# First layer of a two-layer selective scan: states in pairs, softplus passes ahead of the pairs, old y added at the copy

## The chip, the cores and the metric

One core of one Trainium2 chip runs the whole program. The metric is the device time of one execution in microseconds (us). A program on one core is compared by the medians of several executions; the profile is of one further execution of the same kernel.

## The reference, cut to what matters

The input is x, four images of 64 x 64 positions with 192 channels. Two layers follow each other; the change is in the first. It normalizes x, projects it to u (384 channels) and a gate z, and runs a selective scan over the 4096 positions in four directions (by rows, by columns, and both backwards). In each direction there are 384 channels with 16 states each:

```python
def step(h, inp):
    dt, ut, bt, ct = inp
    dA = jnp.exp(dt[..., None] * A_k[None])
    dBu = dt[..., None] * bt[:, :, None, :] * ut[..., None]
    h = dA * h + dBu
    y = jnp.einsum('bkdn,bkn->bkd', h, ct)
    return (h, y)
```

Here dt is the softplus of a small projection, and bt and ct (16 numbers each for every position) are projections too. The four directions' y are summed at their positions, u times D is added, and the sum is normalized, gated with silu(z), projected back to 192 channels and added to x.

## The kernel before, in words

The first layer works image by image ("batch" b = 0 to 3). `between` finishes the image before and projects the next; `scans` (from line 572) does the four directions of one image. The change lies wholly in `scans`.

**Tiling.** An item is one direction k (0 and 2 by rows, forward and backward; 1 and 3 by columns) and one chunk of 512 of the 4096 positions. There are 32 items in an image: first 16 with k = 0 and 2, then 16 with k = 1 and 3. Directions 0 and 2 alternate, and so do 1 and 3. Each item has 16 steps, n = 0 to 15, one for each state; a step works on all 384 channels, as three blocks d of 128 channels on the partitions. All steps of an image make one list `flat`, and g counts through it (512 steps, 2048 in the program).

**What one step does.** For state n of an item:

- ACT makes xT = dt * u * b_n with positions on the partitions (`b_product`, line 716, four ACTIVATE) and the decay a = exp(A dt) (`decay`, line 728, three ACTIVATE).
- PE turns xT, block by block, so that channels lie on the partitions (`turn_x`, line 733; four transposes of 128 x 128 for each d, into one of three PSUM buffers x).
- DVE runs h = a h + x along the 512 positions (`scan`, line 741; three scans of 128 x 512), each starting from the last column of the item before in that direction. After the third, a `tensor_reduce` (line 751) copies the three last columns into the tile carry.
- POOL multiplies h by the row c_n, spread over the partitions by DMA as bct (`c_product`, line 755; 128 x 1536, in place).
- PE turns the product back and adds it in PSUM to the three banks yp (`add_y`, line 768; twelve transposes with accumulation).

**Order.** Each engine's program is written out by hand: the loop over g issues, for every step, first ACT's work for later steps (`b_product(g + 2)`, `decay(g + 1)`), then for d = 0, 1, 2 the scan, the transposes of x for step g + 1 and the adds into y of a state three steps back (LAG = 3), and then the product by c. So on PE an add of state g - 3 stands between the transposes of x for step g + 1. After an item begins, the adds of its first states wait until n = 4, and two states are then added in one step.

**Preparing later items.** Item.steps (line 685) spreads the making of dt and of dt * u for the next two items over the 16 steps: line (ahead, n, engine, function). PE computes dt's projection twice (`dt_rows`, 13 rows into 512 columns; for the item two ahead in steps 7 to 9, for the next item in steps 5 to 7), ACT takes the absolute value and the exponential (steps 10 to 13), POOL has four passes of 128 x 1536: `plus` after the product of step 14 and `minus` after that of step 15 (for the item two ahead), `rest` after the product of step 1 and `total` after that of step 4 (for the next item). ACT takes the logarithm at step 2. DVE forms dt from a PSUM result and these (`delta`, line 661, steps 7 to 9) and dt * u (`times_u`, line 681, steps 11 to 13). In the first eight items of an image the gate's projection is fitted in too (PE and ACT, steps 13 to 15 and following).

**Old y.** The directions are summed in DRAM. Before an item's first add, PE seeds the three banks yp with the old y by a matmul with the identity (`start_y`, line 762: at n = 3 for two banks, n = 4 for the third). The old y of the next item is loaded (tile yold, one buffer) at step 5; only where the next item goes from rows to columns (17th item) is it loaded after the last store of the item before. When an item is done, DVE copies the three banks to the tile yt (`end_y`, line 781) in steps 2 and 3 of the next item, and SP stores yt.

**Buffers.** h has seven tiles of 128 x 1536 (pool b7), a, xT and bct three each, yold, yt, e, wl one each, carry two for each state and direction pair. SP issues all these DMAs in one queue.

Of the kernel before, what the change touches and what calls it, by code (L numbers as in the profile page):

```python
# [12 lines left out]
ALU = mybir.AluOpType  # L13
# [389 lines left out]
class FirstLayer:  # L403
# [168 lines left out]
    def scans(self):  # L572
        nc, tc = self.tc.nc, self.tc
        with ExitStack() as ctx:
            pool = lambda name, bufs, **k: ctx.enter_context(tc.tile_pool(name=name, bufs=bufs, **k))
            p1, p2, p3, p7 = pool("b1", 1), pool("b2", 2), pool("b3", 3), pool("b7", 7)
            pk = pool("ca", 2)
            ps_y = pool("psy", 1, space=bass.MemoryType.PSUM)
            ps_x = pool("psx", 3, space=bass.MemoryType.PSUM)
# [7 lines left out]
            def last(ap, k):  # L587
                return ap[..., LC - 1 : LC] if k < 2 else ap[..., 0:1]
# [15 lines left out]
            class Item:  # L604
# [80 lines left out]
                def steps(self):  # L685

                    s = lambda f, *a: (lambda: f(*a))
                    r = [(3, 12, "pool", self.load_rows), (2, 0, "pe", self.turn_b), (2, 1, "dve", self.keep_b)]
                    for d in range(ND):
                        r += [(2, 7 + d, "pe", s(self.dt_rows, d)), (2, 10 + d, "act", s(self.absolute, d))]  # L690
                    r += [(2, 13, "act", self.exp), (2, 14, "pool", self.plus), (2, 14, "pool", self.load_u)]
                    r += [(2, 15, "pool", self.minus), (1, 2, "act", self.log)]
                    r += [(1, 1, "pool", self.rest), (1, 4, "pool", self.total)]
                    for d in range(ND):
                        r += [(1, 5 + d, "pe", s(self.dt_rows, d)), (1, 7 + d, "dve", s(self.delta, d))]
                    for b in range(ND):
                        r += [(1, 10 + b, "pe", s(self.turn, b)), (1, 11 + b, "dve", s(self.times_u, b))]
                    return r
# [8 lines left out]
                    items += pair if i < NCH // 2 else pair[::-1]  # L707
            flat = [(it, n) for it in items for n in range(NS)]
            N = len(flat)
            carry, xTs, xs, as_, hs, cs = {}, {}, {}, {}, {}, {}  # L710

            def b_product(g):
                it, n = flat[g]
# [22 lines left out]

            def scan(g, d):
                it, n = flat[g]
                if d == 0:
                    hs[g] = p7.tile([128, ND, LC], F32, name="h")  # L740
                nc.vector.tensor_tensor_scan(  # L741
                    along(hs[g][:, d, :], it.k),
                    along(as_[g][:, d, :], it.k),
                    along(xs.pop((g, d)), it.k),
                    0.0 if it.first else carry[it.k, n][:, d : d + 1],
                    ALU.mult,
                    ALU.add,
                )
                if d == ND - 1:
                    kept = carry[it.k, n] = pk.tile([128, ND], F32, name=f"carry{it.k // 2}_{n}")  # L750
                    nc.vector.tensor_reduce(kept, last(hs[g], it.k), mybir.AxisListType.X, ALU.max)  # L751

            def c_product(g):
                it, n = flat[g]
                nc.gpsimd.tensor_tensor(hs[g], hs[g], bc(cs[g - n % 2][:, n % 2, :], 1, ND), ALU.mult)  # L755

            def start_y(it, b):

                if b == 0:
                    it.yp = [ps_y.tile([128, LC], F32, name=f"yp{i}") for i in range(ND)]  # L760
                yo = it.yold.rearrange("p j e -> p (j e)")[:, b * LC : (b + 1) * LC]
                nc.tensor.matmul(it.yp[b], ident, yo, start=True, stop=False, skip_group_check=True)  # L762

            def add_y(g, b):
                it, n = flat[g]
                for i in range(NJ):
                    j, d = divmod(b * NJ + i, ND)
                    nc.tensor.matmul(  # L768
                        it.yp[b][:, i * 128 : (i + 1) * 128],
                        hs[g][:, d, j * 128 : (j + 1) * 128],  # L770
                        ident,
                        start=False,
                        stop=n == NS - 1,
                        is_transpose=True,
                        skip_group_check=True,
                    )

            def end_y(it, b):
                if b == 0:
                    it.yt = p1.tile([128, NJ, DI], F32, name="yt")  # L780
                nc.vector.tensor_copy(it.yt.rearrange("p j e -> p (j e)")[:, b * LC : (b + 1) * LC], it.yp[b])
                if b == ND - 1:
                    for of, to in rows(it.yt, self.y_dram, it.k, it.c):
                        nc.sync.dma_start(to, of)
# [13 lines left out]
            with tc.manual_schedule(engines={nc.tensor.engine, nc.scalar.engine, nc.vector.engine, nc.gpsimd.engine}):  # L798
                tc.keep_in_program_order(nc.scalar.preload_act_table_set("natural_log_exp_and_others"))
                plan = {}  # L800
                for i, it in enumerate(items):
                    for ahead, n, engine, f in it.steps():
                        if i < ahead:
                            f()
                        else:
                            plan.setdefault((i - ahead) * NS + n, []).append((engine, f))
                for t in range(NCH):
                    for e in range(ND):
                        plan.setdefault(t * NS + 13 + e, []).append(("pe", lambda t=t, e=e: gate_in(t, e)))
                        plan.setdefault(t * NS + 15 + e, []).append(("act", lambda t=t, e=e: gate_out(t, e)))  # L810

                def prepare(g, engine):
                    for e, f in plan.get(g, []):
                        if e == engine:
                            f()

                items[0].yold = load("yold", self.y_dram, items[0].k, items[0].c)
                c_rows(0)
                b_product(0)
                b_product(1)  # L820
                decay(0)
                for d in range(ND):
                    turn_x(0, d)
                LAG = 3
                late = []
                for g in range(N + LAG + 1):
                    i, n = divmod(g, NS)
                    it = items[i] if g < N else None
                    before = items[i - 1] if i > 0 else None
                    prepare(g, "act")  # L830
                    if g + 2 < N:
                        if g % 2 == 0:
                            c_rows(g + 2)
                        b_product(g + 2)
                    if g + 1 < N:
                        decay(g + 1)
                    adds = [[] for _ in range(ND)]
                    if it is not None:
                        for at, b in (((LAG, 1), 0), ((LAG, 2), 1), ((LAG + 1, 0), 2)):
                            if at[0] == n:  # L840
                                adds[at[1]].append((start_y, it, b))

                    ready = [x for x in late if x <= g - LAG and (n > LAG or x // NS < i)][:2]
                    for j, (x, b) in enumerate((x, b) for x in ready for b in range(ND)):
                        adds[j // len(ready)].append((add_y, x, b))
                    late = [x for x in late if x not in ready]
                    for d in range(ND):
                        if g < N:
                            scan(g, d)
                        if d == 1:  # L850
                            prepare(g, "dve")
                        if before is not None and (n, d) in ((LAG - 1, 2), (LAG, 0), (LAG, 1)):
                            end_y(before, {2: 0, 0: 1, 1: 2}[d])
                            if (n, d) == (LAG, 1) and it is not None and it.yold is None:
                                it.yold = load("yold", self.y_dram, it.k, it.c)
                        if g + 1 < N:
                            turn_x(g + 1, d)
                        for f, *a in adds[d]:
                            f(*a)
                    if g < N:  # L860
                        prepare(g, "pe")
                        c_product(g)
                        late.append(g)
                        prepare(g, "pool")
                        if n == 5 and i + 1 < len(items) and items[i + 1].k % 2 == it.k % 2:
                            q = items[i + 1]
                            q.yold = load("yold", self.y_dram, q.k, q.c)


    def finish(self, batches):  # L870
# [762 lines left out]
```

## Time and profile before

| | |
|---|---|
| median of 3 executions | 11105.2 us (11085.83 to 11113.26) |
| the profiled execution | 11106.54 us |
| its span, first to last instruction | 11104.6 us |
| granted TensorE clock, mean | 0.939 |
| the four scan stages of the first layer | about 2200 us each, 8793 us together |
| busy over the span | PE 86%, DVE 87%, ACT 88%, POOL 77% |
| scans (L741) | 6144 of 128 x 512, mean 1266 ns (768 without carry: 1207 ns) |
| products by c (L755) | 2048, mean 3470 ns |
| reduces (L751) | 2048, mean 158 ns |
| softplus passes on POOL | 128 each: plus 1478, minus 1482, rest 3460, total 3477 ns |
| seeding of y (L762) | 768 matmul records, 445.1 us busy |
| copies of y (L781) | 384, mean 674 ns |

The page gives for each group of instructions the line, the engine, the operation, what is written and read, the count, the busy time, the mean duration and the idle time of the engine just before it with the instruction that ended it. PE computes in fp32, and a matmul of 512 columns leaves two records. Instructions of one engine overlap a little at their ends, so that the distance from start to start is shorter than the mean duration: five products by c in a row take 17.12 us, 3.42 each. The chain of waits at the end of the span lies in the second layer, and tells nothing of the scan stage; there one reads a window of the timeline instead.

### The profile page before, as it was taken

The page shows a single profiled execution, that of the slowest core. Times are in us where ns is not written, and L with a number is a line of the kernel's source. Part 1 is how long each engine was busy: PE and PEld are TensorE (multiplying, and loading weights), DVE is VectorE, ACT ScalarE, POOL GpSimd, SP SyncE. Part 2 cuts the span into 40 slices and gives each one's busy share as a digit, 9 for nine tenths or more (in the row PEclk, how much of TensorE's full clock was granted, in tenths as well). Part 3 has the DMA queues.
Part 4 walks back from the last instruction along what each step waited for, and adds up shares of the span by engine and source line. Part 5 has one row for each costly group of instructions (what it writes and reads, how often), then busy time and mean ns, then how long its engine had stood idle before and what let it go on. Part 6 is the DMA issues. An engine that isn't in the chain of part 4 may idle for free. (4 is left out here: it accounts for less than half of the span.)

```text
span 11104.6 us, 172135 instructions
## 1 busy us (share of the span) xinstructions
PE 9551.9 (86%) x61449; PEld 7273.6 (66%) x61449; DVE 9693.3 (87%) x11515; ACT 9775.8 (88%) x16979; POOL 8587.9 (77%) x2776
## 2 busy tenths in 40 slices
PE   7998888888988888888988888889988888788677
PEld 4776666666776666656776666657766766655366
DVE  4999899976999899968999899949998999878675
ACT  5999999977999999969999999959999999856477
POOL 3999899955999899938999899929998999700370
PEclk8999999998999999998999999989999999989688
DMA  4333344344333344443333433353333434433458
GB/s 125 109 108 101 91 101 101 98 137 127 109 106 101 92 101 99 98 159 112 109 103 96 98 97 99 93 168 109 109 99 95 98 98 98 120 119 123 157 131 272
DMA packets 833671, 1267.54 MB, mean 114 GB/s; under 512 B 102026, under 2 KB 517655, under 8 KB 832292
## 3 DMA queue, kind: packets, MB, share of 16 engines
q1 hardware_dynamic: 827940, 1250.15, 40.5%
q0 software_dynamic: 4864, 6.29, 0.4%
q8 instruction: 488, 8.00, 0.3%
q14 instruction: 379, 3.10, 0.1%
HBM read 955.83 MB, written 300.42 MB: 113 GB/s over the span
## 5 line engine op out<-in xcount | busy, mean ns | idle before, releaser
L755 POOL TENSOR_TENSOR h<-h,bct 128x1536 f32<-128x1536 f32 x2048 | 7062.9, 3470 | 579.9 <-DVE carry L751 477.5
L741 DVE TENSOR_TENSOR_SCAN h<-a,carry,x 128x512 f32<-128x512 f32 x5376 | 6604.9, 1266 | 231.0 <-PE x L733 194.9
L733 PE MATMUL x<-ident,xT 128*128 128x128 f32 x24576 | 4000.8, 287 | 811.8 <-DVE h L741 710.1
L716 ACT ACTIVATE xT<-dtuT,bT 128x384 f32<-128x384 f32 x8192 | 4358.8, 609 | 93.0 <-PE x L733 87.3
L733 PEld LDWEIGHTS x<-ident,xT 128*128 128x128 f32 x24576 | 2804.0, 145 | 2136.5 <-DVE h L741 920.5
L728 ACT ACTIVATE a<-dt,A_log_f 128x512 f32<-128x512 f32 x6144 | 3977.7, 716 | 0.0
L768 PE MATMUL yp<-ident,h 128*128 128x128 f32 x24576 | 3703.1, 277 | 9.2 <-POOL h L755 9.2
L768 PEld LDWEIGHTS yp<-ident,h 128*128 128x128 f32 x24576 | 2944.2, 144 | 78.8 <-issue 62.6
L632 PE MATMUL dp<-xd,w_dtb_f 13*128 13x512 f32 x1536 | 882.7, 657 | 216.0 <-DVE dt L661 211.3
L741 DVE TENSOR_TENSOR_SCAN h<-a,x 128x512 f32<-128x512 f32 x768 | 899.1, 1207 | 191.3 <-PE x L733 114.0
L645 POOL TENSOR_SCALAR wl<-e 128x1536 f32<-128x1536 f32 x128 | 189.2, 1478 | 799.3 <-ACT e L641 406.2
L519 PE MATMUL pp<-xT,w_in 96*128 96x512 f32 x1152 | 539.2, 617 | 1.1 <-DVE xw L562 1.1
L632 PEld LDWEIGHTS dp<-xd,w_dtb_f 13*128 13x128 f32 x1536 | 235.0, 189 | 456.6 <-DVE dt L661 341.3
L762 PE MATMUL yp<-yold,ident 128*128 128x512 f32 x768 | 445.1, 664 | 72.7 <-DMA yold<-y 72.7
L1137 DVE SCALAR_TENSOR_TENSOR acc<-pad,conv_w_s,acc 128x2048 f32<-128x2048 f32 x192 | 439.3, 2342 | 53.5 <-ACT acc L1135 52.9
L638 ACT ACTIVATE e<-dp 128x512 f32<-128x512 f32 x384 | 224.7, 585 | 269.3 <-DVE dt L661 155.4
L1118 POOL MEMSET pad<- 128x66 f32 x12 | 1.9, 158 | 578.4 <-DVE acc L1137 458.9
L658 POOL TENSOR_TENSOR e<-e,wl 128x1536 f32<-128x1536 f32 x128 | 445.1, 3477 | 0.3
L655 POOL TENSOR_TENSOR e<-e,dt 128x1536 f32<-128x1536 f32 x128 | 442.9, 3460 | 0.3
L751 DVE TENSOR_REDUCE carry<-h 128x3 f32<-128x3 f32 x2048 | 322.7, 158 | 70.4
L519 PEld LDWEIGHTS pp<-xT,w_in 96*128 96x128 f32 x1152 | 221.3, 198 | 244.4 <-issue 234.3
L661 DVE SCALAR_TENSOR_TENSOR dt<-dp,e 128x512 f32<-128x512 f32 x384 | 255.5, 666 | 65.2 <-POOL e L658 58.7
(170 smaller groups left out, 6875.3 us busy)
## 6 DMA issues: line engine op xcount, KB each, us to landing
bct<-xp SPq DMA_DIRECT2D x1024, 512.0 KB, 4.9
uT<-uT SPq DMA_DIRECT2D x64, 768.0 KB, 4.7
yold<-y SPq DMA_DIRECT2D x64, 768.0 KB, 7.9
y<-yt SPq DMA_DIRECT2D x64, 768.0 KB, 4.5
uT<-uT SPq DMA_DIRECT2D x128, 384.0 KB, 5.0
yold<-y SPq DMA_DIRECT2D x128, 384.0 KB, 5.3
y<-yt SPq DMA_DIRECT2D x128, 384.0 KB, 4.6
zg<-gate SPq DMA_DIRECT2D x64, 768.0 KB, 6.3
```

The source lines that it names most:

```text
L519: self.tc.nc.tensor.matmul(pp, self.w_in[:, i, e * 128 : (e + 1) * 128], self.xT[:, i, t * LC : (t + 1) * LC], start=(i == 0), stop=(i == ...
L632: nc.tensor.matmul(self.dp[d], w, self.xd[0 : DR + 1, :], start=True, stop=True)
L655: nc.gpsimd.tensor_tensor(self.e, self.e, self.dt, ALU.subtract)
L658: nc.gpsimd.tensor_tensor(self.e, self.e, self.wl, ALU.add)
L716: nc.scalar.mul(xTs[g][:, j, :], it.dtuT[:, j * DI : (j + 1) * DI], it.bT[:, j, n : n + 1])
L728: nc.scalar.activation(as_[g][:, d, :], it.dt[:, d, :], AF.Exp, scale=scale)
L733: nc.tensor.transpose(xs[g, d][:, j * 128 : (j + 1) * 128], xTs[g][:, j, d * 128 : (d + 1) * 128], ident)
L741: nc.vector.tensor_tensor_scan(along(hs[g][:, d, :], it.k), along(as_[g][:, d, :], it.k), along(xs.pop((g, d)), it.k), 0.0 if it.first els ...
L755: nc.gpsimd.tensor_tensor(hs[g], hs[g], bc(cs[g - n % 2][:, n % 2, :], 1, ND), ALU.mult)
L762: nc.tensor.matmul(it.yp[b], ident, yo, start=True, stop=False, skip_group_check=True)
L768: nc.tensor.matmul(it.yp[b][:, i * 128 : (i + 1) * 128], hs[g][:, d, j * 128 : (j + 1) * 128], ident, start=False, stop=n == NS - 1, is_tr ...
L1137: nc.vector.scalar_tensor_tensor(acc, part(tap), weight(tap), acc, ALU.mult, ALU.add)
```

## The change

Two states that follow each other, n even and n + 1, share one tile h of 128 x 2 x 1536, of which there are three in pool b3. One reduce after the odd state's scans copies the last columns of both (six numbers for each partition). The products by c of both states are issued together, after the odd step. The passes `minus` and `rest` move to the even steps 14 and 2, so that all four passes, which stand in even steps, come ahead of a pair of products on POOL. The seeding matmuls go; the first add of an item writes its bank with the start flag, and `end_y` adds the old y (PSUM and SBUF) where it copied. The old y of an item is loaded at its own step 8, for all items alike.

```diff
-            p1, p2, p3, p7 = pool("b1", 1), pool("b2", 2), pool("b3", 3), pool("b7", 7)
+            p1, p2, p3 = pool("b1", 1), pool("b2", 2), pool("b3", 3)
...
-                    r += [(2, 15, "pool", self.minus), (1, 2, "act", self.log)]
-                    r += [(1, 1, "pool", self.rest), (1, 4, "pool", self.total)]
+                    r += [(2, 14, "pool", self.minus), (1, 2, "act", self.log)]
+                    r += [(1, 2, "pool", self.rest), (1, 4, "pool", self.total)]
...
-                if d == 0:
-                    hs[g] = p7.tile([128, ND, LC], F32, name="h")
+                if d == 0 and n % 2 == 0:
+                    both[g] = p3.tile([128, 2, ND, LC], F32, name="h")
+                    hs[g], hs[g + 1] = both[g][:, 0], both[g][:, 1]
...
-                    0.0 if it.first else carry[it.k, n][:, d : d + 1],
+                    0.0 if it.first else carry[it.k, n - n % 2][:, n % 2, d : d + 1],
...
-                if d == ND - 1:
-                    kept = carry[it.k, n] = pk.tile([128, ND], F32, name=f"carry{it.k // 2}_{n}")
-                    nc.vector.tensor_reduce(kept, last(hs[g], it.k), mybir.AxisListType.X, ALU.max)
+                if d == ND - 1 and n % 2:
+                    kept = carry[it.k, n - 1] = pk.tile([128, 2, ND], F32, name=f"carry{it.k // 2}_{n}")
+                    nc.vector.tensor_reduce(kept, last(both.pop(g - 1), it.k), mybir.AxisListType.X, ALU.max)
...
-            def start_y(it, b):
-
-                if b == 0:
-                    it.yp = [ps_y.tile([128, LC], F32, name=f"yp{i}") for i in range(ND)]
-                yo = it.yold.rearrange("p j e -> p (j e)")[:, b * LC : (b + 1) * LC]
-                nc.tensor.matmul(it.yp[b], ident, yo, start=True, stop=False, skip_group_check=True)
-
             def add_y(g, b):
                 it, n = flat[g]
+                if n == 0 and b == 0:
+                    it.yp = [ps_y.tile([128, LC], F32, name=f"yp{i}") for i in range(ND)]
...
-                        start=False,
+                        start=n == 0 and i == 0,
...
-                nc.vector.tensor_copy(it.yt.rearrange("p j e -> p (j e)")[:, b * LC : (b + 1) * LC], it.yp[b])
+                part = slice(b * LC, (b + 1) * LC)
+                yt, yo = (t.rearrange("p j e -> p (j e)")[:, part] for t in (it.yt, it.yold))
+                nc.vector.tensor_add(yt, it.yp[b], yo)
...
                         prepare(g, "pe")
-                        c_product(g)
+                        if n % 2:
+                            c_product(g - 1)
+                            c_product(g)
                         late.append(g)
                         prepare(g, "pool")
-                        if n == 5 and i + 1 < len(items) and items[i + 1].k % 2 == it.k % 2:
-                            q = items[i + 1]
-                            q.yold = load("yold", self.y_dram, q.k, q.c)
+                        if n == 8:
+                            it.yold = load("yold", self.y_dram, it.k, it.c)
```

## Prediction before the run

> **What bounds the kernel now.** I read the busy rows, then the scan stage of the first layer in windows, then its waits, then the order of time of one item. Columns of a window: length; busy time and count of PE, PEld, DVE, ACT, POOL; PE clock; DMA share; GB/s.
>
> ```profile
> 1500.00:2200.00 700.00, 614.84 (x4304) 482.87 (x4303) 674.17 (x762) 680.92 (x1203) 665.09 (x207) 0.98 0.40 99
> ```
>
> ACT is busy 97%, DVE 96%, POOL 95%, PE 88%: four engines near their limits, so the small waits decide. Those of the same window (total us, times, longest):
>
> ```profile
> POOL h L755 <- DVE carry L751: 34.9, 44, 1.7
> ...
> ACT e L638 <- DVE dt L661: 16.8, 10, 2.0
> ...
> DVE h L741 <- PE x L733: 16.1, 28, 1.0
> ```
>
> ACT waits once an item (1.7 us) and DVE 1.6 us an item, for the transposes of x. I count time by item (16 steps n=0..15) from one last scan to the next. Of the 32 items of a batch 28 are ordinary (not the 1st, 17th, 31st, 32nd): they take 68.5 us on average (69.4 in items 2 to 8, 68.2 later), 67.05 at best. ACT's own work is 16 x 3.87 (four products of B 2.03, three decays 1.84) + 3 x 0.5 + 1.38 + 1.39 = 66.2. DVE's is 16 x 3.765 + 9 x 0.58 + 0.1 = 65.6; the rest is its waits for PE. POOL's is 18 x 3.43 + 2 x 1.45 = 64.6.
>
> The DVE rows show what a reduce costs: a step takes 3.77, and 3.61 without it.
>
> ```profile
> 1772.13 3.62 DVE L741 TENSOR_TENSOR_SCAN h<-a,carry,x 128x512 f32<-128x512 f32 x3
> 1775.78 0.16 DVE L751 TENSOR_REDUCE carry<-h 128x3 f32<-128x3 f32 x1
> 1775.89 3.62 DVE L741 TENSOR_TENSOR_SCAN h<-a,carry,x 128x512 f32<-128x512 f32 x3
> ```
>
> POOL over an item's edge. The product at 1776.17 is step 14's; 1781.04 is step 15's:
>
> ```profile
> 1776.17 3.46 POOL L755 TENSOR_TENSOR h<-h,bct 128x1536 f32<-128x1536 f32 x1 [0.37 <-DVE carry L751]
> 1779.60 1.48 POOL L645 TENSOR_SCALAR wl<-e 128x1536 f32<-128x1536 f32 x1
> 1781.04 3.47 POOL L755 TENSOR_TENSOR h<-h,bct 128x1536 f32<-128x1536 f32 x1
> 1784.46 1.49 POOL L649 TENSOR_SCALAR dt<-wl 128x1536 f32<-128x1536 f32 x1
> 1785.91 6.90 POOL L755 TENSOR_TENSOR h<-h,bct 128x1536 f32<-128x1536 f32 x2
> 1792.78 3.44 POOL L655 TENSOR_TENSOR e<-e,dt 128x1536 f32<-128x1536 f32 x1
> 1796.18 10.31 POOL L755 TENSOR_TENSOR h<-h,bct 128x1536 f32<-128x1536 f32 x3
> 1806.46 3.46 POOL L658 TENSOR_TENSOR e<-e,wl 128x1536 f32<-128x1536 f32 x1
> ```
>
> From step 14 on POOL has no gap until about step 9 of the next item: the four softplus passes put it behind, and the product of state 4 (the third of the 10.31) ends 26.8 us after step 15 (scans ended 1779.71). PE needs it in step 7, from about 30. So POOL's backlog is just covered.
>
> Once a batch (17th item) all engines stop, because the old y is loaded only after the last store and PE needs it first:
>
> ```profile
> PE yp L762 <- DMA yold<-y: 72.7, 4, 18.4
> ```
>
> Those four items take 85.2 us.
>
> **Part by part.** Let t(n) be the end of step n's scans, counted from the end of step 15 of the item before.
>
> Reduces: 8 fewer an item, each worth 0.155 on DVE: -1.24 an item if DVE set the pace. The 128x6 form is not in the trace; it costs between one 128x3 reduce and two (0.16 to 0.32), and I take 0.16, since 3 columns more are little beside 512-column rows of 0.67.
>
> Seeding: 768 matmul records (L762, 445 us of PE) go, from steps 3 and 4, where PE idles 2.4 us an item (step 3). Credit 0 there, but all of the four stops. The copy out of PSUM becomes an add of PSUM and SBUF; the copies are 674 ns, the products of PSUM and SBUF in L681 674 too, so 0 (bounds -0.01 and +0.1 each, at most 38 us). The load of the old y goes past the rows of C and the row loads on SP to step 8 of its own item; it lands in 5.6 us and is needed ten steps later, over 35 us. If that cover were gone it would cost up to 18 us an item. What is queued behind it are rows of C needed two steps later or more.
>
> Buffers: three pairs instead of seven single h. The scan of step g then needs the adds into y of state g-5; these stand on PE ahead of the transposes that this scan needs anyway. 0.
>
> Pairs: the dear part. Behind the waiting product stand on POOL the passes and all later products; PE's adds wait for them, and behind an add stand PE's transposes of x for DVE. POOL may start the pair (12,13) only after step 13, and then has, before PE can use state 4: pairs (12,13), (14,15), (0,1), (2,3) and state 4, nine products at 3.43 = 30.9; the passes, 1.44 + 1.45 + 3.40 + 3.44 = 9.7. Every operand is there earlier (pair (4,5)'s scans end at 24.0), so this runs gapless: 40.6, plus 0.2 from reduce to product. As t(13) is 7.4 before t(15), state 4 ends at 33.4, not 26.8. PE, which carries the adds of states 0 and 1 and two delta matmuls from step 4 on without a gap, reaches it at 30.5 and idles 3.0. Then four transposes (0.44), the next x (0.66) and two signals (0.2): scan (8,1) starts at 34.7, where DVE, with the reduces saved, wanted it at 33.2 (t(7) = 4 x 3.61 + 4 x 3.765 + 0.1 for the copy of B + 3 x 0.585 for the ends of y + 0.58 for one delta = 32.0, and scan (8,0) 1.2). That closes a loop: t(13) -> state 4 -> scan (8,1) -> t(13). Its last leg is 27.4 in an item of the trace (1744.74 to 1772.18), less 0.47 for three reduces, less 1.65 because that item had a slow PE window in step 10 (68.7 against 67.05), plus 0.4 because step 7's two delta matmuls come late too: 25.7. Sum: 0.2 + 40.6 + 1.3 + 25.7 = **67.8 an item with PE at full clock**, against 67.05 now. So DVE's saving is eaten by a stall of 1.5 at step 8.
>
> Slow PE windows: in these two neighbours of 3.41 us PE idles or runs thin 13-row matmuls in the first, and has clock 0.50 in the second:
>
> ```profile
> 1749.72:1753.13 3.41, 2.40 (x15) 1.40 (x14) 3.10 (x4) 1.85 (x5) 3.41 (x2) 1.00 0.20 66
> 1753.13:1756.54 3.41, 3.41 (x18) 3.41 (x17) 2.56 (x2) 3.39 (x7) 3.41 (x2) 0.50 0.65 133
> ```
>
> Today's cost around steps 9 and 10 is 68.2 - 67.05, about 1.1 an item; I keep it: 68.9. The new gap of 3.0 behind a delta matmul should make one more slow window, covering step 7's and 8's transposes: between 0 (bound: it falls where PE has room) and 1.7 (half of 3.41); I take 1.1, the cost of today's. **70.0 an item.**
>
> The Trainium skill, "TensorE: Matmul & The Clock Gate", section "What's actually happening", says PE falls to half rate after at least one idle window of 3413 ns on a free-running grid. By that rule alone a gap of 3.0 us never fills a window and costs nothing, so the sum would be 68.9; the rows above already show a slow window after one that is only 30% idle, and I go by the rows. The skill's "Perfetto Trace Analysis", section "Identifying the Most-Contended Engine", would optimize the engine of highest occupancy first, here ACT, which this change leaves alone; by it only the four stops would go, some -70 us.
>
> Sum: ordinary items (70.0 - 68.5) x 112 = +168. The 17th: (70.0 - 85.2) x 4 = -61. The end of a batch: two products follow the last scan instead of one, +3.4 x 4 = +14. 31st and 32nd about 0. Together +121 on the profiled execution's 11106.5 (span 11104.6), which stands 1.3 above the median of 11105.2: **11227**.
>
> **Rivals.** (a) No new slow window: 68.9 an item. (68.9 - 68.5) x 112 - 16.3 x 4 + 14 = -6: 11100. For it: the gap may straddle two windows; against: a delta matmul lies just ahead of the gap, so about 4 us are thin.
> (b) The faster side: the loop does not bind, because PE's adds of state 4 find slack that I do not see, and ACT becomes the bound from the point where state 4 ends before 32. Items 66.5 (68.1 in the first eight, where ACT has 1.8 more): 21 x 1.7 + 7 x 1.3 = 45 a batch, -180; the stops -74; +14: 10866. For it: only 9.2 us of PE's waits are for POOL today, and the saving on DVE is sure. Against: the gapless rows above.
> (c) Worse: two slow windows an item, or the first half's add waiting for both products (the built program shows separate counts, so hardly): +1.7 to +3.4 an item, 11420 to 11610.
> That the change does not do what it says is excluded by the built order: 1024 reduces, no seeding, passes ahead of the pairs.
>
> **Numbers.** Forecast 0.50, (a) 0.20, (b) or half of it 0.18, (c) 0.12. A measurement of this kernel tells 0.3% from no change. Below 11073: (b) and a third of (a), 0.24. Within: 0.12. Above 11138: forecast, (c) and the edge of (a), 0.64. The range leaves out the far ends of (b) and (c): 11000 to 11380; the forecast's own is 11140 to 11310.
>
> **What would show it.** Right: PE's adds (yp) waiting for POOL h about 2 to 3 us an item in step 7; scans waiting for PE x in step 8; PE clock below 0.97 in the scan stage; no gap on POOL from step 14 to step 9; ordinary items near 70; the 17th like the rest; ACT idle near 3.5 an item. Wrong: ACT idle under 1 an item (rival b), no wait of yp for POOL, or items of 72 and more.

## The result: no change, and the profile after

The changed kernel took 11098.81 us (median of 12 executions, 11080.69 to 11114.39), the kernel before 11101.44 us beside it: ratio 1.0001, 95% interval 0.9993 to 1.0008. The forecast was 11227 us. The profiled execution has a span of 11093.4 us against 11104.6.

The scan stage in a window, columns as before (length; busy time and count of PE, PEld, DVE, ACT, POOL; PE clock; DMA share; GB/s):

```profile
1500.00:2200.00 700.00, 595.97 (x4177) 487.60 (x4176) 656.79 (x675) 674.99 (x1195) 659.25 (x205) 0.94 0.42 99
```

PE, DVE, ACT and POOL are all less busy than before (DVE 657 against 674, ACT 675 against 681) and the PE clock fell from 0.98 to 0.94: DVE's saving is there and is lost again in waits. Those of the same window (total us, times, longest):

```profile
POOL h L756 <- DVE carry L752: 36.6, 20, 3.3
DVE h L742 <- PE x L733: 33.9, 56, 4.1
...
PE yp L764 <- POOL h L756: 26.1, 31, 2.1
ACT e L638 <- DVE dt L661: 21.2, 10, 5.3
```

DVE's waits for PE doubled (16.1 before), and PE now waits for POOL's products, 2.6 us an item, which it did not do before. Over the whole run that wait is 265.8 us against 9.2; the waits of 18.4 us for the old y are gone. The two small operations, with counts, total us and mean ns:

```profile
L779 DVE TENSOR_TENSOR yt<-yp,yold 128x512 f32<-128x512 f32 x384 | 256.2, 667 | 34.3 <-PE yp L764 34.3
L752 DVE TENSOR_REDUCE carry<-h 128x6 f32<-128x6 f32 x1024 | 167.5, 164 | 35.2
```

The add costs what the copy did (674 ns), and the wide reduce what one narrow reduce did (158). POOL over one ordinary item, which begins at 1696.43 where step 15's scans end:

```profile
1689.58 6.90 POOL L756 TENSOR_TENSOR h<-h,bct 128x1536 f32<-128x1536 f32 x2 [1.57 <-DVE carry L752]
1696.43 1.48 POOL L645 TENSOR_SCALAR wl<-e 128x1536 f32<-128x1536 f32 x1
1698.00 1.48 POOL L649 TENSOR_SCALAR dt<-wl 128x1536 f32<-128x1536 f32 x1
1699.44 13.72 POOL L756 TENSOR_TENSOR h<-h,bct 128x1536 f32<-128x1536 f32 x4
1713.12 3.45 POOL L655 TENSOR_TENSOR e<-e,dt 128x1536 f32<-128x1536 f32 x1
1716.53 6.90 POOL L756 TENSOR_TENSOR h<-h,bct 128x1536 f32<-128x1536 f32 x2
1723.38 3.46 POOL L658 TENSOR_TENSOR e<-e,wl 128x1536 f32<-128x1536 f32 x1
1726.81 20.55 POOL L756 TENSOR_TENSOR h<-h,bct 128x1536 f32<-128x1536 f32 x6
```

This is the gapless chain of the prediction. State 4 is the first of the last six: it starts 30.4 us after the item began and ends at 33.8.

Ends of step 15 split the run into items: ordinary 68.97 us on average (68.52 before), the 17th 68.9 (85.2), the 31st 65.9 (65.9), the 32nd 60.5 (62.0), the first 66.0 (66.7). So +0.45 x 112 = +50, -16.3 x 4 = -65, -1.5 x 4 = -6, -0.7 x 4 = -3: -24, which is the difference of the scan stages together (8769 against 8793). Outside them the program is 12 longer, and that this is near the forecast 14 is chance. The second product at each batch's end is there: POOL's last product ends 7.24 us after a batch's last scan instead of 3.79, 13.8 in four batches. But the three stretches from a batch's last scan to the next one's first are 29 longer together, and what follows the fourth batch, for the most part the second layer, is 16 shorter, though the change leaves it alone. Why these stretches differ was not followed.

### The profile page after: what moved, and what is told of

The parts are those of the page before. It is cut to its first block, busy times and chain, and to the rows that moved or that the text cites. A ratio compares the mean times of both kernels' runs of the same rounds, so it can differ in the third digit from the quotient of the medians.

```text
span 11093.4 us, 168325 instructions
## 1 busy us (share of the span) xinstructions
PE 9376.8 (85%) x60681; PEld 7363.0 (66%) x60681; DVE 9534.7 (86%) x10491; ACT 9770.9 (88%) x16979; POOL 8575.4 (77%) x2776
## 5 line engine op out<-in xcount | busy, mean ns | idle before, releaser
L733 PE MATMUL x<-ident,xT 128*128 128x128 f32 x24576 | 4099.6, 292 | 853.0 <-DVE h L742 772.0
L733 PEld LDWEIGHTS x<-ident,xT 128*128 128x128 f32 x24576 | 2913.0, 148 | 1937.3 <-issue 780.5
L764 PE MATMUL yp<-ident,h 128*128 128x128 f32 x24576 | 3838.5, 284 | 265.9 <-POOL h L756 265.8
L764 PEld LDWEIGHTS yp<-ident,h 128*128 128x128 f32 x24576 | 3050.3, 148 | 337.2 <-POOL h L756 337.0
L934 PE MATMUL op<-w_out,v 128*128 128x192 f32 x1536 | 297.1, 345 | 11.3 <-DVE v L924 8.5
L779 DVE TENSOR_TENSOR yt<-yp,yold 128x512 f32<-128x512 f32 x384 | 256.2, 667 | 34.3 <-PE yp L764 34.3
```

The lines of the kernel that those rows point to most:

```text
L733: nc.tensor.transpose(xs[g, d][:, j * 128 : (j + 1) * 128], xTs[g][:, j, d * 128 : (d + 1) * 128], ident)
L764: nc.tensor.matmul(it.yp[b][:, i * 128 : (i + 1) * 128], hs[g][:, d, j * 128 : (j + 1) * 128], ident, start=n == 0 and i == 0, stop=n == N ...
L934: nc.tensor.matmul(op, v[:, d, j * 128 : (j + 1) * 128], w_out[:, d, :], start=(d == 0), stop=(d == ND - 1))
```

## The experiments

In each, a part of the code stands for its whole edit. The granted clock is recorded in windows of 3.41 us, each at 1.00 or at 0.50; one at 0.50 is called a slow window here. Items are sorted by the steps in which the granted clock is 0.50 for over 1 us; "8+9" has it in both, the others go by step 10, then 9, then 8, and what is left has slow windows in steps 3 to 5 at most. Number of the 112 ordinary items, and their mean length:

| kernel | steps 3 to 5 at most | step 8 | step 9 | step 10 | 8+9 | all |
|---|---|---|---|---|---|---|
| before | 20, 67.5 | | 47, 68.1 | 45, 69.4 | | 68.52 |
| after | 63, 67.85 | | 7, 70.4 | 30, 69.9 | 12, 71.7 | 68.97 |
| e6 (step 3 busy) | 30, 67.9 | 2, 69.2 | 3, 68.9 | 12, 70.4 | 65, 71.8 | 70.49 |
| e13 (no gaps on PE) | 112, 68.13 | | | | | 68.13 |
| e3 (plus in step 12) | 25, 67.7 | | 6, 70.7 | 81, 68.6 | | 68.48 |
| e8 (e3, filler in step 8) | 108, 67.50 | | 4, 68.3 | | | 67.53 |

The theory at the start (L): the loop t(13) -> POOL -> state 4 -> scan (8,1) sets 67.8 an item. The rival (R): the loop is not what counts; DVE's work, POOL's total or PE's clock is.

**The two halves of the change.** e1 is the kernel before with old y's part alone (no seeding, the later load, the add), e2 with the pairs, the one reduce and the moved passes alone.

e1 against the kernel before:

```diff
-                nc.vector.tensor_copy(it.yt.rearrange("p j e -> p (j e)")[:, b * LC : (b + 1) * LC], it.yp[b])
+                nc.vector.tensor_add(yt, it.yp[b], yo)
```

e2 against the kernel before:

```diff
-                        c_product(g)
+                        if n % 2:
+                            c_product(g - 1)
+                            c_product(g)
```

> The old y's part alone: no seeding, old y added at the copy, loaded at step 8; states single as before. Theory L (the pairs close a loop on POOL, from the end of step 13 over both pairs, the passes and state 4 to scan (8,1) of the next item; 67.8 us an item with PE at full clock): without pairs there is no loop, the shortest ordinary item is 67.05 as before or a little less, the four stops of some 16 us go; 11030 in all, 11015 to 11050. Rival R (the pairs do no harm; the item is set by DVE and PE as before, and what the reduces save is lost to slow PE windows that the missing seeding brings): the slow windows stand here too, nothing is saved on DVE; 11090 to 11160.

Measured: 11071.03, ratio 0.9969 (0.9957 to 0.9980), between the two. The 17th items fell by 19.3 us as expected, 77 in all, but ordinary items rose to 68.82: PE idles 3.26 us in step 3 instead of 2.42, and all 112 items have slow windows in steps 3 to 5 (30 before). To take 445 us of PE's work away was not free.

> Pairs, one reduce and moved passes alone; seeding and its loads as before. L: shortest ordinary item 67.8 again, the 17th still near 85, PE reaches state 4 at full clock more often, so that more items have the slow window at steps 8 and 9 (71.6): 11150 to 11250. R: without the slow windows of the missing seeding the saved reduces show: items of 66 to 67, 10950 to 11020.

Measured: 11256.43, 1.0130 (1.0113 to 1.0147): the pairs alone cost 1.3%, just above L's range. In the profiled execution (11306.83, the longest of the five) ordinary items are at 69.92; 38 of them have the windows of 8+9 (71.7), 43 slow ones in steps 3 to 5. The two halves don't add up (-33 and +153 us against 0 together): each alters the slow windows of the other.

**The loop's length.** e3 takes the pass `plus` out of the chain (with its exp, to step 12), e4 adds a second one to it. e3 against the changed kernel:

```diff
-                    r += [(2, 13, "act", self.exp), (2, 14, "pool", self.plus), (2, 14, "pool", self.load_u)]
+                    r += [(2, 12, "act", self.exp), (2, 12, "pool", self.plus), (2, 14, "pool", self.load_u)]
```

What e4 adds after `plus` in step 14, against the changed kernel:

```diff
+                    nc.gpsimd.tensor_scalar(self.wl, self.e, 1.0, 1.0, ALU.add, ALU.mult)
```

> As changed, but the exponential and the pass plus stand in step 12 instead of 13 and 14, so that plus fills POOL's gap ahead of the pair (12,13) and leaves the loop. L: the loop is 1.45 shorter, the shortest ordinary item 66.4 (ACT's own work, 66.2, is next): 10940 to 10980. R: POOL does not set the item, 67.8 stays: 11090 to 11110.

Measured: 11039.56, 0.9943 (0.9926 to 0.9960), between the two ranges. The four 18th items are at 65.9, 1.4 under those of the changed kernel (67.3), as L has it. But apart from them no item after a batch's ninth is without a slow window from step 7 on; 81 got one in step 10 and stand at 68.6: of the 1.4 an item that L gives, 0.5 is left (68.48).

> As changed, with the pass plus run twice in step 14 (same result): 1.45 more on POOL within the loop. L: every ordinary item is 1.45 longer, shortest 69.25; 11099 + 1.45 x 116 = 11267, 11230 to 11300. R: POOL has 4 us of idle time an item, so nothing: 11090 to 11120.

Measured: 11310.35, 1.0187 (1.0170 to 1.0204). The 40 items without a slow window from step 7 on have a median of 69.52, 1.7 more than those of the changed kernel (67.82), and all ordinary ones stand at 70.60. The pass is paid in full, and more.

> As changed, with one more POOL pass of 1.45 (dt into a spare tile that nobody reads) in step 10, outside the loop, where POOL waits for the pair (10,11). It is the control to the pass run twice in step 14, which cost 1.9 an item. L: nothing, 11090 to 11115. A theory in which POOL's work as a whole counts: 1.45 x 120 more, 11240 to 11290.

The pass of e5 stands in step 10, outside the loop:

```diff
+                        if n == 10 and i + 2 < len(items):
+                            nc.gpsimd.tensor_scalar(spare, it.dt, 1.0, 1.0, ALU.add, ALU.mult)
```

Measured: 11071.37, 0.9970 (0.9960 to 0.9979). It costs nothing; POOL's idle time falls from 4.25 to 2.87 an item. So POOL's total is not the bound, only what lies in the loop. Why it is 0.3% below the changed kernel isn't shown: of the 29 us between the two profiled executions 10 lie in the scan stages, and between the batches it is 34 shorter, after the fourth 16 longer.

**The missing slow window.** e6 keeps PE busy in step 3, into a PSUM tile that nothing reads:

```diff
+                        if it is not None and n == LAG:
+                            if d == 0:
+                                idle = ps_m.tile([128, LC], F32, name="idle", tag="m")
+                            nc.tensor.matmul(idle, ident, it.dtuT[:, d * LC : (d + 1) * LC], start=True, stop=True)
```

> As changed, with three matmuls of 512 columns (dt times u into a PSUM tile that nobody reads) in step 3, where the seeding stood. Theory W (the predicted slow PE window behind the gap at state 4 stays out because PE is already slow in steps 4 and 5, after its idle step 3, and comes to state 4 late): PE now comes early, the gap at step 7 is 2 to 3 again and about a third of the items have the slow window at steps 8 and 9 (71.6); 11150 to 11230. Rival: the gap makes no slow windows, and those of steps 4 and 5 cost time themselves: 11040 to 11100.

Measured: 11274.63, 1.0148 (1.0127 to 1.0170): filling an idle engine made the kernel 1.5% slower. No item has a slow window in steps 3 to 5 any more; PE reaches state 4 at full clock and waits 2.4 us (median; 1.2 in the changed kernel), and 65 of 112 items get the slow windows in steps 8 and 9. PE in such an item of e6, then the windows around:

```profile
1752.01 0.66 PE L733 MATMUL x<-ident,xT 128*128 128x128 f32 x4
1755.05 0.66 PE L764 MATMUL yp<-ident,h 128*128 128x128 f32 x4 [2.38 <-POOL h L756]
...
1758.37 3.78 PE L632 MATMUL dp<-xd,w_dtb_f 13*128 13x512 f32 x4
```

```profile
1752.88:1756.29 3.41, 1.24 (x11) 1.25 (x12) 2.02 (x4) 3.41 (x7) 3.41 (x2) 1.00 0.97 213
1756.29:1759.71 3.42, 3.42 (x13) 2.57 (x12) 3.01 (x3) 3.37 (x7) 3.42 (x2) 0.50 0.15 20
1759.71:1763.12 3.41, 3.41 (x8) 1.39 (x8) 0.00 (x0) 1.94 (x4) 3.41 (x2) 0.50 0.61 186
1763.12:1766.53 3.41, 3.41 (x18) 3.41 (x17) 2.81 (x3) 0.00 (x0) 2.06 (x1) 0.50 0.00 2
```

After the window in which PE was busy 1.24 of 3.41 come three at half clock, not one, though PE is busy all through them; the slowed 13-row delta matmuls (3.78 us) lie in the first two. DVE stands still for a whole window, and step 9's scans wait:

```profile
1763.30 1.28 DVE L742 TENSOR_TENSOR_SCAN h<-a,carry,x 128x512 f32<-128x512 f32 x1 [4.00 <-PE x L733]
```

The changed kernel's item from above, in the same view:

```profile
1708.33:1711.74 3.41, 1.09 (x9) 0.65 (x8) 3.18 (x4) 3.41 (x8) 3.41 (x2) 1.00 0.57 104
1711.74:1715.16 3.42, 2.48 (x10) 1.72 (x11) 3.39 (x5) 3.42 (x8) 3.42 (x2) 0.50 0.10 37
1715.16:1718.57 3.41, 3.41 (x18) 3.41 (x17) 3.16 (x3) 3.41 (x7) 3.41 (x2) 0.50 0.87 285
...
1728.81:1732.22 3.41, 1.98 (x19) 1.92 (x19) 2.65 (x4) 3.41 (x7) 3.41 (x2) 1.00 0.85 171
1732.22:1735.64 3.42, 3.42 (x19) 2.00 (x18) 2.66 (x4) 3.42 (x8) 3.42 (x2) 1.00 0.21 77
```

```profile
1730.30 0.66 PE L764 MATMUL yp<-ident,h 128*128 128x128 f32 x4 [1.43 <-POOL h L756]
```

Here PE is thin in step 3 (1.09 of 3.41), is slow in steps 4 and 5, comes to state 4 late and waits only 1.43 for its product; that window keeps 1.98 busy, and the next stays at full clock. The slow windows that cost nothing prevent those that would cost four. That they cost nothing in the changed kernel is seen from its items after the ninth without a slow window from step 7 on: with under 4.5 us of slow clock before it they have a median of 67.83 (9 items), with more 67.81 (36).

**What ties the two states.** e7 gives each state its own reduce again and still issues the products in pairs:

```diff
-                if d == ND - 1 and n % 2:
+                if d == ND - 1:
...
+                    nc.vector.tensor_reduce(kept[:, n % 2], last(hs[g], it.k), mybir.AxisListType.X, ALU.max)
```

> As changed, but each state has its own reduce again (128x3, 1024 more), products still in pairs. L: DVE waits 1.3 at step 8 anyway, so the reduces ahead of that are free; only those of steps 8, 10, 12, between scan (8,1) and the loop's end, count: +0.47 an item at most, 11110 to 11155. If DVE's work set the item: 8 x 0.155 = 1.24 an item, 11240.

Measured: 11084.81, 0.9979 (0.9970 to 0.9989), below what either expected. POOL in e7:

```profile
1538.22 3.50 POOL L761 TENSOR_TENSOR h<-h,bct 128x1536 f32<-128x1536 f32 x1 [0.68 <-DVE carry L755]
1543.29 3.48 POOL L761 TENSOR_TENSOR h<-h,bct 128x1536 f32<-128x1536 f32 x1 [1.58 <-DVE carry L755]
1547.80 3.49 POOL L761 TENSOR_TENSOR h<-h,bct 128x1536 f32<-128x1536 f32 x1 [1.03 <-DVE carry L755]
```

The products run singly, each after its own reduce, and state 4 ends 30.06 us into the item (median) instead of 33.85. I had taken the order of issue for the tie; it is the one reduce. So e7 has no loop, and PE doesn't wait for state 4 in any ordinary item. It still lies near the changed kernel, because 98 of its 112 items have slow windows in step 9 or 10, and ordinary items reach 69.07 (17th items 65.1). The 14 others have a median of 67.04, 0.8 under the 67.82 of the loop.

**Slow windows of steps 9 and 10.** PE waits there for delta. e8 adds a matmul of zeros to an accumulating bank in step 8 of e3; e9 does so in the changed kernel, e10 in the one before, e11 in e7 (e9 to e11 with a broadcast column for the zeros):

```diff
+            zero = p1.tile([128, LC], F32, name="zero")
+            nc.vector.memset(zero, 0.0)
...
+                        if n == 8:
+                            nc.tensor.matmul(it.yp[0], ident, zero, start=False, stop=False, skip_group_check=True)
```

> The kernel with plus and the exponential in step 12, and one matmul of 512 columns that adds zeros to y's first bank in step 8, just where PE idles 1.0 behind the wait for delta. Theory W: the window with that gap and thin matmuls is no longer idle enough, the slow windows of steps 9 and 10 go (72 items of 128 had one there, 68.05 against 65.9): 10870 to 10940. Rival: slow windows do not come from what PE did in the window before: 11030 to 11060.

Measured: 10906.35, **0.9823** (0.9807 to 0.9840), the fastest kernel of all, 1.8% under both. Of the 81 items with a slow step 10 none is left. For e8, the stretch of the scan stage and three of its waits, in the views shown above for the changed kernel:

```profile
1500.00:2200.00 700.00, 613.67 (x4324) 492.02 (x4322) 668.90 (x690) 689.67 (x1219) 673.24 (x209) 0.96 0.42 100
```

```profile
POOL h L758 <- DVE carry L754: 20.8, 12, 2.0
DVE h L744 <- PE x L735: 19.8, 44, 0.8
ACT e L640 <- DVE dt L663: 9.9, 8, 1.6
```

ACT is busy 690 of 700; its wait for delta has halved, DVE's longest wait for x fell from 4.1 to 0.8, and PE's for POOL's product is no longer among the great ones. L's 66.4 is reached in part: of the items after the ninth without a slow window from step 7 on, 23 with under 4.5 us of slow clock before it have a median of 66.31, 53 with more 67.38. Where the loop is shorter, the slow windows of steps 3 to 5 do cost.

> The changed kernel, with one matmul of 512 columns that adds zeros to yp[0] in step 8, where PE waits for delta. Loop theory (the loop over POOL, state 4 and the scan of step 8 sets 67.8 an item wherever PE runs at full clock, and the slow windows of steps 9 and 10 come on top): the windows of steps 9 and 10 go, items stand at 67.8, a few with windows in steps 8 and 9 still at 71.6; ordinary items 68.0 to 68.4 on average, 10985 to 11045 us. Rival (those slow windows cost nothing, since the loop holds DVE up anyway): 11085 to 11115.

Measured: 11024.09, 0.9939 (0.9922 to 0.9955), as L has it: 87 items at 68.1 (median 67.84), 25 with a slow step 8, 68.37 on average.

> The kernel before, with the same zero-adding matmul in step 8; its four stops in the 17th items stay. Loop theory: without the slow windows of steps 9 and 10 the old order has no loop, ordinary items stand at 67.05 to 67.4, 10950 to 11000 us, so that the changed kernel with the same filler is 20 to 50 us dearer than this one, although it lacks 65 us of stops. Rival (the change itself costs nothing in ordinary items): this kernel about 65 us above the changed one with the filler.

Measured: 11075.19, 0.9982 (0.9972 to 0.9992); L missed, and the rival has it nearly. The windows of step 10 went, but 48 items keep one in step 9 (68.6), and the others rose from 67.1 to 67.75 (medians), as the filler itself delays PE: the delta projection behind it ends 0.8 us later in the item. Ordinary items are at 68.38, those of e9 at 68.37. So beside the old order with the same filler, and not at its best of 67.05, the changed kernel's ordinary items cost nothing more.

> The changed kernel with a reduce for each state, so that each product waits for its own state alone, and with the filler in step 8. Loop theory: no loop and no windows in steps 9 and 10, ordinary items 66.8 to 67.3, 10855 to 10925 us, faster than the changed kernel with the filler by over 90 us. DVE theory (the saved reduces are what helps): no faster than the changed kernel with the filler, since 8 reduces of 0.155 an item are back (139 us).

Measured: 10999.18, 0.9912 (0.9895 to 0.9928): 25 below e9, not over 90; L missed. Without the loop ordinary items are at 68.23. Those without a slow window from step 7 on have a median of 68.20, against 67.04 in e7: as in e10, the filler costs where there is no loop to cover it. What sets 68.2 there isn't shown; ACT waits for delta 1.4 an item, as much as in e9.

> The kernel with exp and plus in step 12 and the filler in step 8, with three more matmuls of 512 columns to an unused tile in step 3, so that PE comes to state 4 at full clock. Window theory (PE then waits long for state 4 in step 7, and this gap makes slow windows in steps 8 and 9, +3.9 in some 40 to 70% of the items): ordinary items 68.0 to 69.1, 10960 to 11090 us, slower than without the added matmuls (10906). Rival (all slow windows only cost, so fewer in steps 3 to 5 are a gain): items at 66.4, 10780 to 10850 us.

e12 is e8 with the matmuls of e6. Measured: 10923.64, 0.9842 (0.9826 to 0.9858), between the two. 57 items have a slow window in step 8, but only one, and it costs 1.6, not 3.9: their median is 67.92, and the 21 items after the ninth that have none lie at 66.28. That is L's 66.4, 1.5 under the changed kernel's 67.82.

**PE without gaps.** e13 is e9 with e6's matmuls and three more that add zeros ahead of state 4's adds; e14 does so to e12; e15 gives the kernel before two matmuls in step 3 and two fillers in step 8.

e13 against e9, beside the lines of e6:

```diff
+                        if it is not None and (n, d) == (7, 0):
+                            for _ in range(3):
+                                nc.tensor.matmul(it.yp[0], ident, zero.to_broadcast([128, LC]), start=False, stop=False, skip_group_check=True)
```

> The changed kernel with PE kept busy in its three gaps: three matmuls of 512 columns to an unused tile in step 3, three that add zeros to yp[0] ahead of state 4's adds in step 7, one more in step 8. Loop theory: hardly a slow window is left in steps 3 to 10 and nearly all ordinary items stand at 67.8 (67.7 to 68.1 on average), 10950 to 10995 us. Window theory (PE's slow windows alone set both kernels, there is no loop): items at 66.3 to 67.0, 10790 to 10870 us.

Measured: 11002.93, 0.9907 (0.9890 to 0.9923), 8 above L's range. The same stretch of e13, and two of its waits:

```profile
1500.00:2200.00 700.00, 633.46 (x4390) 484.67 (x4388) 660.55 (x680) 681.03 (x1207) 667.79 (x207) 1.00 0.43 100
```

```profile
POOL h L758 <- DVE carry L754: 31.4, 20, 1.9
DVE h L744 <- PE x L735: 30.0, 42, 1.4
```

The clock is 1.00, not one of the 112 items has a slow window, and their median is 67.84: the loop as it was worked out, to 0.1%. The mean, 68.13, is raised by the first eight items of a batch (68.9), which carry the gate's work. But PE doesn't wait for state 4 here. In an item whose state 4 ends at 4117.80 on POOL (the first of the six products) the added matmuls fill just that gap:

```profile
4114.36 20.55 POOL L758 TENSOR_TENSOR h<-h,bct 128x1536 f32<-128x1536 f32 x6
4115.31 2.75 PE L857 MATMUL yp<-zero,ident 128*128 128x512 f32 x6
4117.89 0.62 PE L766 MATMUL yp<-ident,h 128*128 128x128 f32 x4
```

So e13 alone doesn't tell the loop from the added matmuls. The 30 items of e6 without a slow window do: PE waits for state 4's product in all of them (0.4 to 2.4 us), and their median is 67.84 as well.

> The same fillers on the kernel with exp and plus in step 12. Loop theory: ordinary items at 66.4 (66.3 to 66.9 on average), 10790 to 10860 us, 1.4 an item under the changed kernel with the same fillers. Window theory: equal to it, 10790 to 10870 us both.

Measured: 10936.24, 0.9845 (0.9828 to 0.9861): 67 us below e13, not 155. The median is 67.26, not 66.4; the fillers ahead of state 4 now stand in PE's way: it waits for POOL's product in no ordinary item, and state 4's first add begins 1.1 us (median) after its product is there.

> The kernel before with PE kept busy in its gaps: two matmuls of 512 columns to an unused tile in step 3, two that add zeros in step 8. Its four stops stay. Loop theory: no loop, ordinary items at 67.05 (67.0 to 67.6 on average), 10935 to 11005 us; 0.2 to 1.0 an item less than the changed kernel with its fillers. Window theory: items equal to those of the changed kernel with its fillers, so 65 us above it by the stops.

Measured: 11228.04, 1.0108 (1.0091 to 1.0125): above both ranges. Behind the second filler ACT waits longer for delta (2.2 us an item, 1.4 in the kernel before), and 75 items still have a slow step 9, 12 of them with step 8. So the old order at full clock throughout was not seen; its 67.05 rests on the 15 items of the kernel before without a slow window.

## Why the prediction was wrong

- **The loop: right.** 67.8 an item were worked out from single rows; items of the changed kernel without a slow window from step 7 on have a median of 67.82, those of e6 without one anywhere 67.84. State 4 ends at 33.85 against 33.4. A pass of 1.45 less in the loop made items without slow windows 1.5 shorter (66.28 in e12), one more made them 1.7 longer (e4), and one outside it cost nothing (e5). (Its tie is the single reduce, not the order of issue, as e7 showed; the prediction's sum is not touched by that.)
- **The stops, the small parts: right.** 17th items at 68.9, -65 us (forecast -61); POOL's second product at the batch ends +14 (+14), though the stretches outside the scan stages moved by more than that for reasons not followed; the add, the wide reduce and the load of old y at no cost.
- **The new slow PE window, +1.1 an item: the step that failed.** It was priced at one window in every item. Measured are three windows and 3.9 us, in 12 of 112 items: 46 us, 0.4 an item. And the 1.1 that I kept for the windows of steps 9 and 10 is 0.75 now: (30 x 2.1 + 7 x 2.6 + 63 x 0.05) / 112. Together 1.16 where I had 2.2: ordinary items +50 us instead of +168, which is 118 of the 132 between forecast and profiled execution. The rest lies in the 17th, 32nd and first items. With the term at zero the sum is rival (a), 11100; that it meets the measured time is partly luck, since its 1.1 for the old windows stands where 0.75 of old and 0.41 of new ones were measured.
- **Why it failed.** I let PE reach state 4 at 30.5, at full clock. But the seeding whose removal I credited with 0 had kept PE busy in step 3. Without it PE's idle time there rose from 2.42 to 3.17 an item, all 112 items have slow windows in steps 3 to 5 (30 before), and PE comes late: the gap at state 4 is 1.2 (median), not 3.0. (The rest of PE's waits for POOL, 0.8 an item, is for the last products of the item before.) e6 undoes just that and brings the forecast windows in 65 items. The prediction had used the rule that a partly idle window makes a slow one for step 7 only, and not for step 3, where its own change thinned PE's work.
- The Trainium skill, "TensorE: Matmul & The Clock Gate", section "What's actually happening", says that half rate comes after at least one idle window of about 3.4 us. By it a gap under 3.41 costs nothing. The sum came out near what that would give, but not for that reason: windows with 1.09 and 1.24 busy of 3.41 were followed by half clock here, one with 1.98 was not.

How much work keeps the clock can be read from the traces in the main. A window with 2.40 busy had a slow one after it in the kernel before, one with 1.98 none here; but 1.12 of the 2.40 were thin 13-row matmuls. All windows in the scan stages of the 17 profiles were sorted by PE's busy time without the 13-row matmuls. Of those at clock 1.00 with 1.75 us or more, 1 of 35678 was followed by clock 0.50; with under 1.25, 1007 of 1020; between, 1358 of 3016. With the 13-row matmuls counted in, 791 of the 37929 with 1.75 or more were. This is a sorting of runs made for other ends; 13-row matmuls were not varied by themselves.

What stays open: why the stretches between the batches differ, and what holds the items of e11 at 68.2. Nor was the whole old order seen without slow windows.

## What to carry to other kernels

Where a clock follows an engine's activity, work taken off that engine has a price: look at the window in which it stood, not only at the end of the queue, and then follow the engine's later arrival to the next wait. A loop across items (here from a shared reduce through a queue and back to the scan that feeds it) can be summed from single rows to 0.1%, and can set the pace though no engine is full. If slow windows stand behind gaps, a matmul of zeros into an open accumulation, put where the engine waits anyway, may be worth more than the tuning: 1.2% from e3 to e8. Where the engine has little to wait for, the filler takes back part of what it saves (e10, 0.2% faster) or more than that (e15, 1.1% slower).

## What the runs showed of the hardware

Slow windows can follow each other though PE is busy: after one thin window (1.24 us of 3.41) PE ran 10.2 us at half clock, busy all through. Thin 13-row matmuls filled part of the first two of these three windows, and without them PE was busy 2.15 and 1.05. That fits all other windows at clock 0.50 in the scan stages of the 17 profiles: with under 2.5 us busy without the 13-row matmuls, none of 1002 was followed by full clock; with more, 2434 of 2873 were.

The position of slow windows in an item keeps to a few patterns: item lengths of the changed kernel gather at 67.8, 69.5 and 71.65. A small edit can move the time by favouring one of them, as e6 did.
